# Additions of a two-level Strassen product: bank folding in the first pass, and p7's and the weights' outer sums moved from VectorE to GpSimd

## The chip, the cores and the metric

The kernel runs on one core of a Trainium2 chip. The metric is the device time of one execution in microseconds (us); it is the time of the slowest core, and here there is only one. TensorE multiplies matrices into banks of PSUM, VectorE, ScalarE and GpSimd work on elements, and SyncE issues most of the transfers. GpSimd does not touch PSUM in this kernel: whatever comes from a bank goes through VectorE or ScalarE.

## The reference, cut to what matters

Two layers follow each other over 2048 tokens (8 x 256) of width 512. The first adds to the normalised input a linear attention with 32 heads and a mixture of 16 experts; the second adds a plain attention and a low-rank mixture. The change lies in the first layer's attention, in its projections:

```python
qkv = jax.nn.silu(hidden_states @ qkv_w.T)        # 512 -> 3 * 32 * 128
scores = einsum('bhnd,bhmd->bhnm', cq, ck) * diag_decay
intra = einsum('bhnm,bhmd->bhnd', scores, cv)
xf = xf * rsqrt(mean(xf * xf) + EPS)
gate = jax.nn.sigmoid(hidden_states @ gate_w.T)   # 512 -> 32 * 128
return gate * normed @ out_w.T
```

Everything is in 32-bit floats. The four projections q, k, v and gate are one product of the tokens with a weight matrix of 512 x 16384.

## The kernel before

**Passes, units, halves.** The tokens are taken in two passes (`i` = 0, 1) of 1024 tokens. In each pass there are 8 units (`g`), one for each group of 4 heads, and each unit has two halves (`h`): h = 0 makes q and k, h = 1 makes the gates and v. A half is one large matrix product, tokens by weights.

**Two levels of Strassen.** That product is done by Strassen's scheme in Winograd's form, with seven products in place of eight, on two levels. The outer level has the products p1, p2, p6, p5, p3, p7, p4 (`ORDER`); each is an object `Outer` and is itself made of seven inner products with the same names, done in the order p1, p7, (p3 of the outer product before), p6, p4, p2, p5. So there are 2 x 8 x 2 x 7 = 224 outer products, and each inner one is two matmuls of 128 x 128 x 256 in the code (line 872; the records of the profile show two per matmul). The inner products of one outer product accumulate in three kinds of bank: `ps_a` (two of them), `ps_b` and `ps_e`. p1's sum is copied out of bank a (`c1`) before p6 is accumulated onto it, p6's sum likewise (`c2`) before p5, and p7's sum out of bank e (`c3`) before p4. The copy is `copied` (line 1203), the use of the sums is `result` (line 1212).

**What becomes of a result.** An outer product gives four quarters (`q` = 0 to 3, of 128 x 512). They go into four tiles a, b, c, d: p1 makes a; p2 makes b = a + result; p6 is added to a; p5 makes c = a + result; p3 makes d = c + result; p7 is added both to c and to a; p4 is added to a. When b, d, c and a are whole, `Part.begin` starts what follows for them: the silu (h = 0) or the gate (h = 1) on ScalarE, then scores, the weighing of v, the gating (`gT`, line 1016) and the projection back by `w_out`.

**The third operand.** In three of the four quarters a result is the sum of a bank, a copy of an earlier bank and a tile. In the second pass (`u.i` is 1) the tile is already added when the first bank is copied: VectorE writes bank + tile into `cp` (line 1207, by the helper of line 103), and `result` adds the second bank to it. `folded` (line 1199) says which: p2, p6, p5, p4 with a, p3 with c, but not p4's quarters 0 and 3. In the first pass ScalarE copies the bank (line 1209), VectorE adds the second bank, and GpSimd adds the tile, for p2, p5 and p3 straight onto the new tile (`c<-c`), for p6 and p4 by way of a tile `r` (`c<-c,r`).

**p7.** For each of its quarters a tile r = bank + copy is made; GpSimd adds it to c, and VectorE adds it to a (`add_a`, line 1174). For quarter 1 there is no copy, and r is a copy by ScalarE (line 1235).

**Weights.** In the first pass the sums of the weights that both levels need are made on the way, in the tile `w` of the next outer product, by `weights` (line 824); the result of the inner level is stored, and the second pass loads it. `outer_sum` makes sums over a whole quarter, in two pieces of 128 x 512; p6 has four such additions, p3 and p7 have two each, the others none. `inner_sum` makes four sums of 128 x 256 for each outer product, three on VectorE and the fourth on GpSimd. Each step has the name of an inner product of the current outer product behind which it is issued: the outer sums behind p1 and p7, the inner ones behind p7, p6, p6 and p2.

**What sets the order.** VectorE, ScalarE and GpSimd run in the order in which the program issues (`manual_schedule`). Pieces of other work (scores, projections, experts, table transfers) are put between inner products by `later` and `slot` (lines 877 to 888), and a piece is due a number of slots after the one where it was put. TensorE's order is made by the planner from its own costs. The transfers are issued by SyncE, some by ScalarE, the indirect ones by GpSimd. Tiles come from rings: 5 of `cp`, 4 of `sum` (r), 16 of `S`.

Of the kernel before, what the change touches and what calls it, by code (L numbers as in the profile page):

```python
# [73 lines left out]
def block_kernel(  # L74
# [24 lines left out]
    nc = tc.nc  # L99
    mm = nc.tensor.matmul  # L100

    def tt(o, a, b, op, eng=None):
        (eng or nc.vector).tensor_tensor(o, a, b, op)  # L103
# [298 lines left out]
    def add(o, a, b, eng=None):  # L402
        tt(o, a, b, ALU.add, eng)
# [134 lines left out]
    at = NTT * E  # L538
# [257 lines left out]
    with tc.tile_pool(name="attn", bufs=1) as attn, tc.manual_schedule(engines={mybir.EngineType.Activation, mybir.EngineType.Pool, mybir.EngineType.DVE}):  # L796
# [27 lines left out]
        def weights(i, g, h, p, steps):  # L824

            w = loaded[p].pop(0)
            y = w[:, 0:4]
            v = nc.vector
            pool = nc.gpsimd
            kept = ws[2 * g + h][p]  # L830
            if i == 0:
                latest[p] = y

                def outer_sum(f, o, a, b, n):
                    f(o[:, n : n + 2], a[:, n : n + 2], b[:, n : n + 2], v)

                def inner_sum(f, o, a_, b_):
                    f(w[:, o], w[:, a_], w[:, b_], pool if o == 6 else v)
                    if o == 6:
                        later(6, store)  # L840

                def store():
                    nc.scalar.dma_start(out=kept, in_=w[:, 4 if p in RAW else 1 : 8])

                outer = []
                if p == "p6":
                    w5 = loaded["p5"][0]
                    outer = [(add, w5, w5, w5[:, 4:8]), (sub, y, w5, y)]
                elif p == "p3":
                    outer = [(sub, y, y, latest["p6"])]  # L850
                elif p == "p7":
                    outer = [(sub, y, y, w[:, 4:8])]
                for n, when in ((0, "p1"), (2, "p7")):
                    steps += [(when, partial(outer_sum, *at, n)) for at in outer]
                steps += [
                    (when, partial(inner_sum, *at)) for when, at in (
                        ("p7", (sub, 7, 1, 0)), ("p6", (add, 4, 0, 3)), ("p6", (sub, 5, 4, 1)), ("p2", (sub, 6, 2, 5))
                    )
                ]
            return dict(zip(("p1", "p2", "p4", "p5", "p6", "p3", "p7"), (w[:, n] for n in range(1, 8))))  # L860
# [16 lines left out]
        def later(after, f):  # L877
            pieces.append((now[0] + after, len(pieces), f))
            pieces.sort(key=lambda x: x[:2])
# [292 lines left out]
            places_of.update(a=b, b=d, c=c, d=a)  # L1172

        def add_a(a, r):
            add(a, a, r)

        class Outer:


            def __init__(self, unit, h, p):  # L1180
                self.u, self.h, self.p = unit, h, p
                self.steps, self.added = [], []
                self.following = None
                self.w = weights(unit.i, unit.g, h, p, self.steps)
                self.x = first_x.pop(0) if first_x else tokens(unit.i, p, tc.keep_in_program_order)
# [12 lines left out]

            def folded(self, q):

                return self.u.i and (self.p, q) not in (("p4", 0), ("p4", 3)) and {"p2": "a", "p5": "a", "p6": "a", "p4": "a", "p3": "c"}.get(self.p)

            def copied(self, bank, q):
                c = attn.tile([P, 512], FP, tag="cp", name="cp", bufs=5)
# [7 lines left out]
            def result(self, i, j, bank, c):  # L1212

                u, p, q = self.u, self.p, 2 * i + j
                pool = nc.gpsimd
                a = u.tile(self.h, "a")[:, q]
                made, with_ = dict(
                    p1=("a", None), p2=("b", "a"), p5=("c", "a"), p3=("d", "c")
                ).get(p, (None, None))
                if made:  # L1220
                    o = u.tile(self.h, made)[:, q]
                    if c is None and with_ is None:
                        nc.scalar.copy(o, bank)
                    elif c is None:
                        add(o, bank, u.tile(self.h, with_)[:, q])
                    else:
                        add(o, bank, c)
                        if with_ and not self.folded(q):
                            add(o, o, u.tile(self.h, with_)[:, q], pool)
                elif p != "p7" and (c is None or self.folded(q)):  # L1230
                    add(a, bank, a if c is None else c)
                else:
                    r = attn.tile([P, 512], FP, tag="sum", name="r", bufs=4)
                    if c is None:
                        nc.scalar.copy(r, bank)  # L1235
                    else:
                        add(r, bank, c)
                    if p != "p7":
                        add(a, a, r, pool)
                    else:  # L1240
                        c_ = u.tile(self.h, "c")[:, q]
                        add(c_, c_, r, pool)

                        self.added.append(partial(add_a, a, r))
                        if (i, j) == (1, 1):
                            for n in range(3):
                                later(n, self.added.pop(0)) if n else self.added.pop(0)()
                        elif (i, j) == (0, 1):
                            self.added.pop(0)()
                whole = dict(p2=("b", 0, 0), p3=("d", 0, 1), p7=("c", 1, 1), p4=("a", 1, 0)).get(p)  # L1250
                if whole and (i, j) == (0, 1):
                    Part(u, self.h, whole[1], whole[2], u.tile(self.h, whole[0])).begin()
# [228 lines left out]
        for n, (i, g, h, p) in enumerate(plan):  # L1481
            cur = outers[n]
            u = cur.u
            k = ORDER.index(p)
            at = 2 * (i * NG + g) + h
# [381 lines left out]
```

## Time and profile before

| | |
|---|---|
| three runs | 2711.66, 2715.54 and 2711.70 us, median 2711.7 |
| the profiled execution | 2719.83 us, of which the span is 2718.1 |
| TensorE busy in the span | 2637.7 us (97%) |
| VectorE busy | 1915.6 us (70%) |
| GpSimd busy | 1401.4 us (52%) |
| ScalarE busy | 850.6 us (31%) |
| first pass of the attention | from 131 us to about 1224 us |
| second pass | to about 2380 us |

The profile has one execution. Its groups give, for a line, an engine, an operation and its tiles (out<-in), the number of instructions, their busy time and the mean of one in ns, then the engine's idle time in front of them and what ended it. The table of waits adds up that idle time by who waited and for whom: total in us, times, longest. In the timeline a line has the start and the length in us; equal neighbours are merged (x2). PE is TensorE, PEld its weight loads, DVE VectorE, ACT ScalarE, POOL GpSimd, SP SyncE. Nearly all additions have line 103, a helper, so they are told apart by their tiles and shapes.

### The profile page before, as it was taken

To read this page: it belongs to the slowest core of one execution; us is meant where nothing else is said; L and a number is where in the kernel's file an instruction comes from. 1 tells how busy PE (TensorE), PEld (TensorE's weight loads), DVE (VectorE), ACT (ScalarE), POOL (GpSimd) and SP (SyncE) were. 2 spreads that over 40 slices of the span, in tenths; PEclk is the share of its full clock that TensorE was granted. 3 is DMA by queue.
4 is the path that set the end of the run, shared out by engine and by line. 5 is a ranking of instruction groups with operands and counts; after the bars stand their busy time and mean duration, and the time that the engine had idled before them with its cause. 6 is when DMAs were issued, how large, how long until landed. Compare 5 with 4: busy or idle time off the path is not lost. (4 is left out here: it accounts for less than half of the span.)

```text
span 2718.1 us, 38734 instructions
## 1 busy us (share of the span) xinstructions
PE 2637.7 (97%) x14218; PEld 2296.1 (84%) x14218; DVE 1915.6 (70%) x3193; ACT 850.6 (31%) x1249; POOL 1401.4 (52%) x1294
## 2 busy tenths in 40 slices
PE   8999999999999999999999999999999999989999
PEld 5588888888989898988889888888989888967777
DVE  8697777778787787766556565766666676847663
ACT  4234343434343434332322122222312232321121
POOL 7458686868685857664433334252433443362210
PEclk8999999999999999999999999999999999999999
DMA  6798676767777777776768586867767686533211
GB/s 249 296 382 296 243 284 245 282 244 284 251 276 259 271 274 259 278 281 235 269 228 288 210 296 218 291 236 251 272 228 280 245 302 217 205 118 116 79 48 64
DMA packets 163120, 655.62 MB, mean 241 GB/s; under 512 B 19776, under 2 KB 22336, under 8 KB 160960
## 3 DMA queue, kind: packets, MB, share of 16 engines
q1 hardware_dynamic: 125936, 499.16, 52.1%
q10 hardware_dynamic: 21024, 92.81, 8.4%
q0 software_dynamic: 15968, 61.13, 6.7%
q8 instruction: 115, 1.88, 0.3%
q14 instruction: 77, 0.63, 0.1%
HBM read 512.13 MB, written 143.78 MB: 241 GB/s over the span
## 5 line engine op out<-in xcount | busy, mean ns | idle before, releaser
L872 PE MATMUL ps_a<-xt,w 128*128 128x256 f32 x2688 | 718.5, 382 | 9.9 <-ACT cp L1209 4.0
L872 PEld LDWEIGHTS ps_a<-xt,w 128*128 128x128 f32 x2688 | 470.8, 191 | 67.2 <-issue 10.3
L103 POOL TENSOR_TENSOR c<-c,r 128x512 f32<-128x512 f32 x256 | 352.8, 1393 | 239.9 <-DVE r L103 220.7
L1069 PE MATMUL ps_sc<-wo,gT 128*128 128x256 f32 x1792 | 424.2, 380 | 4.5 <-DVE gT L1016 3.0
L1209 ACT COPY cp<-ps_a 128x512 f32<-128x512 f32 x304 | 177.5, 584 | 676.5 <-PE ps_a L872 582.5
L1069 PEld LDWEIGHTS ps_sc<-wo,gT 128*128 128x128 f32 x1792 | 335.2, 191 | 49.5 <-DVE gT L1016 3.5
L872 PE MATMUL ps_e<-xt,w 128*128 128x256 f32 x1344 | 366.7, 382 | 6.5 <-DVE c L103 6.5
L103 POOL TENSOR_TENSOR sums<-sums,sq 128x256 f32<-128x256 f32 x240 | 195.9, 816 | 327.8 <-ACT sq L1007 318.2
L103 DVE TENSOR_TENSOR w<-w 128x256 f32<-128x256 f32 (+1 forms) x464 | 353.0, 769 | 5.4
L872 PEld LDWEIGHTS ps_a<-w,xt 128*128 128x128 f32 x1792 | 270.5, 191 | 23.0
L872 PE MATMUL ps_a<-w,xt 128*128 128x128 f32 x1792 | 272.2, 274 | 0.0
L103 POOL TENSOR_TENSOR c<-c 128x512 f32<-128x512 f32 x144 | 191.4, 1340 | 146.5 <-DVE c L103 138.2
L872 PEld LDWEIGHTS ps_e<-xt,w 128*128 128x128 f32 x1344 | 232.8, 192 | 32.5 <-DVE c L103 8.0
L103 DVE TENSOR_TENSOR acc<-ps_sc,acc 128x512 f32<-128x512 f32 x196 | 134.7, 688 | 146.5 <-PE ps_sc L1069 145.8
L1016 DVE SCALAR_TENSOR_TENSOR gT<-ps_o,nw,c 128x256 f32<-128x256 f32 x256 | 111.9, 478 | 151.2 <-ACT sq L1007 127.4
L872 PE MATMUL ps_b<-xt,w 128*128 128x256 f32 x672 | 182.6, 380 | 0.0
L103 DVE TENSOR_TENSOR c<-c,r 128x512 f32<-128x512 f32 x128 | 170.9, 1366 | 4.9 <-ACT r L1235 4.9
L103 POOL TENSOR_TENSOR gT<-gT 128x512 f32<-128x512 f32 x128 | 170.3, 1331 | 3.8 <-DVE gT L1016 1.3
L103 DVE TENSOR_TENSOR s<-ps_sc,decay 128x384 f32<-128x384 f32 x256 | 139.9, 552 | 43.0 <-PE ps_sc L984 42.1
L103 DVE TENSOR_TENSOR c<-ps_a,c 128x512 f32<-128x512 f32 x160 | 109.7, 686 | 85.5 <-PE ps_a L872 84.7
L1007 ACT ACTIVATE sq<-ps_o 128x512 f32<-128x512 f32 x128 | 76.6, 599 | 285.3 <-PE ps_o L997 260.7
L996 PE MATMUL ps_o<-s,c 128*128 128x256 f32 x512 | 157.3, 389 | 8.8 <-DVE gT L1016 8.5
(291 smaller groups left out, 4369.5 us busy)
## 6 DMA issues: line engine op xcount, KB each, us to landing
xt<-xc SPq DMA_DIRECT2D x224, 896.0 KB
w<-in_w_att_dram SPq DMA_DIRECT2D x144, 512.0 KB
w<-in_w_att_dram SPq DMA_DIRECT2D x48, 384.0 KB
wo<-in_w_out_dram SPq DMA_DIRECT2D x56, 256.0 KB
decay<-dec SPq DMA_DIRECT2D x32, 384.0 KB
yd<-ye SPq DMA_DIRECT2D x36, 256.0 KB
wos<-wo ACTq DMA_DIRECT2D x32, 256.0 KB
wo<-wos SPq DMA_DIRECT2D x32, 256.0 KB
```

Source lines behind the costliest of these rows:

```text
L103: (eng or nc.vector).tensor_tensor(o, a, b, op)
L872: mm(o, a, b, start=(first and ty == 0), stop=True, skip_group_check=True)
L996: mm(po[:, bass.ts(hh, S)], v[:, 0:P], s[:, 0:S], start=True, stop=False)
L1007: nc.scalar.activation(sq, po, AF.Square)
L1016: nc.vector.scalar_tensor_tensor(gT[:, h, :], po[:, bass.ts(h, S)], nw[:, n : n + 1], self.c[:, 2 * h + t, 0:S], ALU.mult, ALU.mult,)
L1069: mm(py[:, bass.ts(t, S)], self.O[l, p][:, hh, bass.ts(t, P)], self.wo[p][:, hh, :], start=(t == 0 and hh == 0), stop=(hh == 1), skip_grou ...
L1209: nc.scalar.copy(c, bank)
```

## The change

It has four parts. `folded` no longer asks for the second pass, so in the first pass too the third operand is added by VectorE when the first bank is copied. The outer sums of the weights are issued to GpSimd. The additions of p7's results to a are issued to GpSimd, in both passes; and for quarter 1 of p7, where there is no copy, VectorE adds the bank straight to c and then to a, in both passes. For outer products whose weights have outer sums (p6, p3, p7) the inner sums are issued one inner product later: behind p6, p4, p2 and p5.

```diff
-                    f(o[:, n : n + 2], a[:, n : n + 2], b[:, n : n + 2], v)
+                    f(o[:, n : n + 2], a[:, n : n + 2], b[:, n : n + 2], pool)
...
+                whens = ("p6", "p4", "p2", "p5") if outer else ("p7", "p6", "p6", "p2")
                 steps += [
-                    (when, partial(inner_sum, *at)) for when, at in (
-                        ("p7", (sub, 7, 1, 0)), ("p6", (add, 4, 0, 3)), ("p6", (sub, 5, 4, 1)), ("p2", (sub, 6, 2, 5))
+                    (when, partial(inner_sum, *at)) for when, at in zip(
+                        whens, ((sub, 7, 1, 0), (add, 4, 0, 3), (sub, 5, 4, 1), (sub, 6, 2, 5))
                     )
                 ]
...
         def add_a(a, r):
-            add(a, a, r)
+            add(a, a, r, nc.gpsimd)
...
-                return self.u.i and (self.p, q) not in (("p4", 0), ("p4", 3)) and {"p2": "a", "p5": "a", "p6": "a", "p4": "a", "p3": "c"}.get(self.p)
+                return (self.p, q) not in (("p4", 0), ("p4", 3)) and {"p2": "a", "p5": "a", "p6": "a", "p4": "a", "p3": "c"}.get(self.p)
...
                 elif p != "p7" and (c is None or self.folded(q)):
                     add(a, bank, a if c is None else c)
+                elif p == "p7" and c is None:
+                    c_ = u.tile(self.h, "c")[:, q]
+                    add(c_, bank, c_)
+                    add(a, bank, a)
                 else:
```

## Prediction

> **What bounds the kernel now.** I read the stages first: the busy time by stretches, here from 204 us to the end of the first pass at about 1224 us, and the second pass to 2380 us.
>
> ```profile
> core 0: us, PE busy (x) PEld busy (x) DVE busy (x) ACT busy (x) POOL busy (x), PEclk, DMA share, GB/s
> 204.00:1224.00 1020.00, 1002.84 (x5551) 901.58 (x5550) 796.53 (x1216) 394.48 (x573) 729.11 (x659) 1.00 0.75 269
> 1224.00:2380.00 1156.00, 1138.24 (x6516) 1016.90 (x6514) 757.29 (x1159) 315.50 (x436) 455.57 (x430) 1.00 0.71 251
> ```
>
> TensorE is idle 17.2 us of the first pass and 17.8 us of the second. No edit here takes a matmul away, so those gaps are nearly all that can be won. What ends them is in the table of waits of TensorE, first pass and then second:
>
> ```profile
> PE ps_o L996 <- DVE gT L1016: 8.5, 8, 1.4
> PE ps_e L872 <- DVE c L103: 6.5, 8, 1.2
> PE ps_a L872 <- DVE r L103: 1.5, 4, 0.4
> PE ps_sc L983 <- DVE s L103: 6.0, 3, 2.5
> PE ps_sc L1069 <- DVE gT L1016: 3.0, 1, 3.0
> ```
>
> All of these name VectorE, though it is busy only 78% and 66%. So it is late at certain places. The timeline around one gap of each pass shows why. First pass (start, duration, instruction):
>
> ```profile
> 378.03 2.35 DVE L103 TENSOR_TENSOR w<-w 128x256 f32<-128x256 f32 x2
> 378.65 1.45 POOL L103 TENSOR_TENSOR c<-c,r 128x512 f32<-128x512 f32 x1
> 380.13 1.06 ACT L965 ACTIVATE c<-c 128x1024 f32<-128x1024 f32 x1 [4.03 <-POOL c L103]
> 383.69 0.60 ACT L1007 ACTIVATE sq<-ps_o 128x512 f32<-128x512 f32 x1
> 384.32 0.88 DVE L1016 SCALAR_TENSOR_TENSOR gT<-ps_o,nw,c 128x256 f32<-128x256 f32 x2 [1.55 <-ACT sq L1007]
> 385.34 0.73 PE L996 MATMUL ps_o<-s,c 128*128 128x256 f32 x1 [1.37 <-DVE gT L1016]
> ```
>
> Read it upwards: the matmul waits for gT, gT for the square, the square stands behind the gate on ScalarE, and the gate waited 4.03 us for p7's last addition to c on GpSimd. Second pass:
>
> ```profile
> 1413.94 6.78 DVE L103 TENSOR_TENSOR c<-c,r 128x512 f32<-128x512 f32 x2
> 1414.63 4.93 POOL L103 TENSOR_TENSOR c<-c,r 128x512 f32<-128x512 f32 x4
> 1420.64 0.54 DVE L103 TENSOR_TENSOR s<-ps_sc,decay 128x384 f32<-128x384 f32 x1
> 1421.24 0.48 PE L983 MATMUL ps_sc<-c 128*128 128x256 f32 x1 [2.52 <-DVE s L103]
> ```
>
> Two VectorE additions with both operands in SBUF took 6.78 us while GpSimd ran four of its own; alone one takes 0.67 us. The scores stood behind them and a matmul behind those. Additions that read PSUM took 0.68 us beside the same kind of GpSimd work.
>
> **The change part by part.** Groups of the first pass:
>
> ```profile
> L103 DVE TENSOR_TENSOR w<-w 128x512 f32<-128x512 f32 x128 | 124.3, 982 | 1.1
> L103 DVE TENSOR_TENSOR c<-c,r 128x512 f32<-128x512 f32 x64 | 78.0, 1248 | 0.0
> L103 POOL TENSOR_TENSOR c<-c 128x512 f32<-128x512 f32 x144 | 191.4, 1340 | 146.5 <-DVE c L103 138.2 <-issue 8.2
> L1209 ACT COPY cp<-ps_a 128x512 f32<-128x512 f32 x226 | 131.9, 584 | 463.1 <-PE ps_a L872 371.3 <-DMA xr<-x 22.7 <-DVE w L103 22.2
> ```
>
> *Third operand with the first bank (first pass).* Per half 3 copies each in p2, p6, p5, p3 and 1 in p4 become VectorE additions: 13 x 16 = 208, at 0.688 us (the second pass's cp<-ps_a,c) +143 us on VectorE, -122 us on ScalarE (0.585 each). GpSimd loses 144 c<-c (-191 us) and 4 x 16 = 64 additions of r for p6 and p4 (-90 us, 1.40 each); the results that wrote r now write a, at the same price.
>
> *Outer sums to GpSimd.* 128 additions leave VectorE (-124 us) and cost GpSimd 128 x 1.34 = +172 us.
>
> *p7.* 64 additions to a per pass leave VectorE: -78 us and, second pass, 64 x 1.484 = -95 us. Per p7 three go to GpSimd, the fourth quarter is added from its bank twice on VectorE, and one copy of ScalarE and one addition to c go. Per pass: VectorE +32 x 0.688 = +22 us, GpSimd 48 - 16 = 32 more at 1.40, +45 us.
>
> Sums: VectorE -37 us in the first pass and -73 in the second; GpSimd -64 (-191 - 90 + 172 + 45) and +45; ScalarE -131 and -9. Neither engine is the bound by totals, so only lateness counts. SP's order and its DMAs stay; on GpSimd's queue the outer sums now stand among the indirect DMAs of the table (1.02 us each) and wait for weights to land, with c, a and sums behind them. At 131 to 204 us that queue had long gaps.
>
> A rule against the change: the Trainium skill, "GPSIMD Engine Reference", Engine selection, gives elementwise additions to VectorE and calls GpSimd about twice as slow. The trace agrees (1.27 against 0.67 us); by the rule alone the outer sums are a loss of 128 x 0.6 = 77 us, by the stage totals nothing, since GpSimd keeps 29% idle.
>
> What goes on the path:
> - ps_o 8.5 us: c is finished by GpSimd's third addition (374.97 + 1.3 = 376.3) and VectorE's from the bank, so the gate starts some 3 us earlier. 1.37 us of wait is covered twice: -8.5.
> - ps_e 6.5 and ps_a 1.7 (1.5 and a row of 0.2): before 362.96 VectorE had outer sums and others of 3.23 us (357.28); they go: -8.
> - Second pass: additions like 6.78 us above stand before 1421, 1575 and 1730, and one of 5.35 us at 2231 before the wait of 3.0: -9.
> - Slow restart: after 385.34 four matmuls take 1.43 us where 1.03 is usual, and the clock is 0.97 in two stretches of 68 us (about 2 us each): -1.5, between 0 and -4.
>
> What comes:
> - Start: p2's first copy was made by ScalarE at 140.67; VectorE does the routing sums until 144.8, and the product p6 that needs the bank ran about 144: +2, between 0 and +4.
> - Copies behind VectorE's queue: in the bare outer products p6 and p5 of h=1 (ps_b at 472.24, 478.38, 484.30: 6.1 and 5.9 us) VectorE has 7 additions from PSUM at 0.60 us spacing and 3 of weights at 0.43, 5.5 us where it had 3.7. A copy has two products (1.76 us) to be done in and needs about 1. The far end is one blocked addition in SBUF (2.16 us at 349.74, 1.7 over a free one): 16 x 0 to 1.7. I take 0.4, near the second pass, where TensorE barely waits for cp (1.1 us in all): +6.
> - New wait: p4's copy of quarter 2 now needs GpSimd's addition to a. From r at 447.6: three to c, one of weights, one to a = 4 x 1.27 + 0.73 = 5.8, so 453.4; the product that needs the copy starts at 455.61, so 1.5 us are left after the copy's 0.69. Behind the waiting copy stand scores and weights, and p5 on TensorE. At 32 places 0 to 0.7 (one addition blocked 2.16 us ahead of it, less 1.5); I take 0: the 1.5 us that stay are more than the 1.27 of one GpSimd addition.
>
> Sum: -8.5 - 8 - 9 - 1.5 + 2 + 6 = -19. The profiled execution took 2719.8 us (span 2718.1 and 1.7 around it), so 2700.8; the median of the runs is 8.1 lower: **2693 us**.
>
> **Rivals.**
> *Slower: GpSimd's sums block the weights in front of the copies.* In p2, p5 and p3 VectorE's inner sums have both operands in SBUF and now run beside the outer sums that feed them. A blocked one waits for one GpSimd addition, 1.3 us, with a copy behind it; less the slack of about 0.3 that is 1 us of TensorE, at 3 x 16 = 48 places: +48 - 27 (all gains but the start) + 2 = +23: 2735. It decides from 0.5 us at each. For it: w<-w 128x256 at 0.69 on average, not 0.43, and 2.35 for two at 378.03. Against: they start a product later, and of the outer products only two a unit are bare (others take 8 to 16 us).
> The Trainium skill, "SBUF — State Buffer", Who interferes with whom, says that a VectorE instruction with two SBUF inputs and a GpSimd one that reads SBUF exclude each other for a whole instruction. The trace agrees at 1413.94 (6.17 us for the first of two).
> *No gain: the gaps move.* TensorE, no longer held here, comes to weights that have not landed (DMA share 0.75), or the new waits give 20 us back: 2707 to 2717, say 2711. Against: waits for DMA cost it 1.4 us before 204 us and none after in the first pass.
> *It does not do what it says*: the list of instructions shows the 208 and 128 moved; 0.
>
> **Numbers.** Forecast 0.64, no gain 0.13, slower 0.23. A change under 0.2% (5.4 us) can't be told from none here: faster 0.64, same 0.13, slower 0.23. The likeliest case alone spans 2682 (2693 less the 6 and 2 that come and 2.5 more of restart) to 2706; the range goes 4 lower, the spread of the runs shown (2711.66 to 2715.54), to 2678, and up to 2727, most of the way to the slower case, leaving out about 0.1 above and 0.1 below.
>
> **What would show it.** Right: no ps_o<-gT and ps_e<-c waits over 0.5 us from 204 to 1224, no s wait at 1421, ScalarE's L965 not waiting for GpSimd, TensorE idle under 12 us in that pass. Wrong: TensorE waiting for cp in p2, p5, p3, or VectorE's cp for GpSimd's a at p4, over 0.5 us each time; or weights' inner sums over 1 us on average.

## The result, and the profile after

The changed kernel takes 2696.76 us (median of four runs, 2694.35 to 2698.81), the kernel before 2713.19 beside it: a ratio of 0.9938, 95% interval 0.9921 to 0.9956, so 16.4 us faster. Forecast were 2693 us and a range of 2678 to 2727. The profiled execution took 2695.74 us, with a span of 2693.9.

Waits of TensorE in the profile after, the same stretches as before, first the first pass (204 to 1224 us), then the second (total us, times, longest):

```profile
PE ps_e L873 <- DVE c L103: 7.3, 8, 1.1
PE ps_a L873 <- DVE c L103: 1.0, 5, 0.2
```

```profile
PE ps_sc L913 <- DMA xw<-xnd,whose: 8.8, 2, 5.8
PE ps_sc L1070 <- PEq L1324: 1.5, 1, 1.5
PE ps_sc L1070 <- issue: 1.3, 1, 1.3
PE ps_a L873 <- DVE cp L103: 0.4, 1, 0.4
```

The waits for gT and for s are gone. The wait for c in bank e, forecast to go, is there once a unit as before, 7.3 us after 6.5. In these stretches of the first pass TensorE waits for no copy `cp`.

The groups of the first pass that the change touches:

```profile
L103 DVE TENSOR_TENSOR w<-w 128x256 f32<-128x256 f32 x330 | 184.2, 558 | 22.5 <-POOL w L103 17.8 <-DMA ws61p<-w 2.6
L103 DVE TENSOR_TENSOR cp<-ps_a,c 128x512 f32<-128x512 f32 x150 | 103.0, 686 | 37.4 <-PE ps_a L873 31.9 <-POOL w L103 4.7
L103 POOL TENSOR_TENSOR w<-w 128x512 f32<-128x512 f32 x128 | 162.1, 1274 | 16.5 <-DMA w<-in_w_att_dram 13.7
```

The outer sums cost GpSimd 1274 ns each; the inner ones on VectorE are shorter than before (558 after 693 ns), but VectorE now waits for GpSimd in front of some of them: 17.8 us.

For an account by stages I take the starts of TensorE's products into bank b in each profiled execution, which are the same products in every kernel, and subtract those of the profiled execution before:

| | before, us | change after |
|---|---|---|
| first unit of the first pass | 121.0 | +2.5 |
| its units 2 to 8 | 941.4 | -15.6 |
| second pass | 1174.8 | -8.1 |
| all around them | 481.0 | -3.0 |

The last row has none of the changed instructions, and ten of the thirteen changed kernels (this one and those below) are 1.1 to 5.1 us shorter there: the execution of before that was profiled seems to have taken longer in it than usual. So of the 24.2 us between the two spans 21 belong to the change at most. Each stage is from one execution per kernel; differences of a few us in a stage are not shown to be there in the times.

### The profile page after: what moved, and what is told of

The parts are those of the page before. It is cut to its first block, busy times and chain, and to the rows that moved or that the text cites. A ratio compares the mean times of both kernels' runs of the same rounds, so it can differ in the third digit from the quotient of the medians.

```text
span 2693.9 us, 38333 instructions
## 1 busy us (share of the span) xinstructions
PE 2629.2 (98%) x14218; PEld 2295.1 (85%) x14218; DVE 1780.0 (66%) x3209; ACT 713.0 (26%) x1009; POOL 1308.3 (49%) x1278
## 5 line engine op out<-in xcount | busy, mean ns | idle before, releaser
L103 POOL TENSOR_TENSOR c<-c,r 128x512 f32<-128x512 f32 x256 | 322.8, 1284 | 229.0 <-DVE r L103 228.5
L103 POOL TENSOR_TENSOR sums<-sums,sq 128x256 f32<-128x256 f32 x240 | 180.1, 750 | 360.7 <-ACT sq L1008 350.8
L103 POOL TENSOR_TENSOR w<-w 128x512 f32<-128x512 f32 (+1 forms) x240 | 242.3, 1019 | 211.4 <-DVE w L103 178.8
L103 DVE TENSOR_TENSOR cp<-ps_a,c 128x512 f32<-128x512 f32 x288 | 198.1, 688 | 73.3 <-PE ps_a L873 61.6
L1210 ACT COPY cp<-ps_a 128x512 f32<-128x512 f32 x160 | 93.4, 584 | 539.9 <-PE ps_a L873 517.2
L103 DVE TENSOR_TENSOR c<-ps_a,c 128x512 f32<-128x512 f32 x224 | 150.9, 685 | 82.6 <-PE ps_a L873 81.7
L103 DVE TENSOR_TENSOR w<-w 128x256 f32<-128x256 f32 x336 | 186.9, 556 | 22.5 <-POOL w L103 17.8
```

Of the source, the lines that this page charges most:

```text
L1210: nc.scalar.copy(c, bank)
```

## The experiments

Three parts (the fold; p7; the outer sums on GpSimd with their later inner sums) give eight kernels with the two known ones. Each ratio is to runs of the kernel before that were taken beside it, and the last three columns are the differences by stage, as in the table above.

| kernel | ratio (95% interval) | median, us | unit 1 | units 2-8 | second pass |
|---|---|---|---|---|---|
| all (the change) | 0.9938 (0.9921-0.9956) | 2696.8 | +2.5 | -15.6 | -8.1 |
| p7 alone | 0.9884 (0.9868-0.9900) | 2686.3 | -2.9 | -15.2 | -12.3 |
| fold alone | 1.0001 (0.9991-1.0011) | 2715.1 | +0.9 | -1.4 | -1.5 |
| weights alone | 1.0205 (1.0188-1.0222) | 2771.9 | +11.3 | +46.6 | -1.0 |
| without p7 | 1.0011 (1.0000-1.0022) | 2718.7 | +2.9 | -4.3 | -1.1 |
| without the weights | 0.9919 (0.9899-0.9938) | 2692.1 | -0.5 | -13.1 | -14.2 |
| without the fold | 1.0149 (1.0134-1.0164) | 2758.1 | +8.6 | +43.5 | -11.7 |

### p7 alone

```diff
-            add(a, a, r)
+            add(a, a, r, nc.gpsimd)
...
+                elif p == "p7" and c is None:
+                    c_ = u.tile(self.h, "c")[:, q]
+                    add(c_, bank, c_)
+                    add(a, bank, a)
```

> The kernel before with one part alone: p7's additions to a on GpSimd, and quarter 1 of p7 added from its bank to c and to a by VectorE, in both passes. By my theory the second pass loses its waits for s and gT behind VectorE additions with both operands in SBUF (9 us), and the first pass gains a few us at the most where VectorE is relieved of 78 us, since the gate still waits for GpSimd's c: 2713 - 9 - 3 = 2701 us, 2697 to 2707. By the rival that the fold is the gain: 2713 us, and the waits of the second pass only move.

2686.3 us: some 30 us faster than before, faster than the range of 2697 to 2707, and faster than the whole change. The second pass gives 12.3 us where 9 were expected, the first 18 where 3 were. TensorE's waits in its units 2 to 8 (254 to 1224 us) are the wait for bank e and little else:

```profile
PE ps_e L872 <- DVE c L103: 5.3, 7, 1.2
PE ps_a L872 <- DVE c L103: 0.3, 1, 0.3
```

So the wait for gT went with p7's edits, without any fold. The expectation had kept it ("the gate still waits for GpSimd's c"), although the prediction's own step for it rests on quarter 1 being added from its bank, which is part of p7.

### One half of p7, and the other

Quarter 1 direct, with the other additions to a left on VectorE:

```diff
+                elif p == "p7" and c is None:
+                    c_ = u.tile(self.h, "c")[:, q]
+                    add(c_, bank, c_)
+                    add(a, bank, a)
```

> The kernel before with half of the p7 part: quarter 1 of p7 is added from its bank to c and to a by VectorE; p7's other additions to a stay on VectorE. p7's part alone took 29 us. My theory is that its gain in the first pass (18 us) comes from this half: c no longer waits for a copy by ScalarE and an addition by GpSimd, the gate starts earlier, and the wait of TensorE for gT goes with the slow matmuls behind it; its gain in the second pass (12 us) comes from the other half. So about -14 to -18 here: 2699 us, 2695 to 2704. The rival is that the first pass gains by the relief of VectorE from additions in SBUF, most of which stay here: then -5 at the most, 2708 to 2714.

2696.6 us, ratio 0.9929 (0.9915 to 0.9943), within the range expected: these four lines alone give the time of the whole change. By stages: unit 1 -1.9, units 2 to 8 -16.4, second pass -4.1. Its timeline at the place of the gap (start, duration, instruction) shows how the gate is reached:

```profile
375.93 1.28 DVE L103 TENSOR_TENSOR c<-ps_a,c 128x512 f32<-128x512 f32 x2
376.70 1.06 ACT L965 ACTIVATE c<-c 128x1024 f32<-128x1024 f32 x1 [1.56 <-DVE c L103]
```

The gate starts 0.1 us after the first of the two additions from the bank has ended, where before it waited for a copy on ScalarE, a queue on GpSimd and an addition there.

The other half, all four additions to a on GpSimd and quarter 1 as before:

```diff
-            add(a, a, r)
+            add(a, a, r, nc.gpsimd)
```

> The kernel before with the other half of the p7 part: p7's additions to a are GpSimd's, all four quarters, and quarter 1 still goes by way of ScalarE's copy and GpSimd. By my theory the second pass gains its 9 to 12 us (no VectorE addition with both operands in SBUF is left in it to be blocked), and the first pass keeps the wait for gT, perhaps 1 us longer each time, since GpSimd has more to do ahead of c: 2715 - 11 + 4 = 2708 us, 2702 to 2714. By the rival that relief of VectorE is the gain in both passes: 2690 to 2697.

2756.2 us, ratio 1.0147 (1.0130 to 1.0163): some 40 us slower, where 7 less than before was expected. Both theories missed it. Waits of its first pass, units 2 to 8, and the timeline of one:

```profile
PE ps_o L996 <- DVE gT L1016: 23.1, 6, 4.2
PE ps_sc L983 <- ACT c L960: 8.1, 7, 1.3
```

```profile
378.22 5.51 POOL L103 TENSOR_TENSOR c<-c,r 128x512 f32<-128x512 f32 x4
378.37 0.59 ACT L1235 COPY r<-ps_a 128x512 f32<-128x512 f32 x1
383.69 1.53 POOL L103 TENSOR_TENSOR sums<-sums,sq 128x256 f32<-128x256 f32 x2
385.18 4.94 POOL L103 TENSOR_TENSOR c<-c,r 128x512 f32<-128x512 f32 x4
386.48 1.06 ACT L965 ACTIVATE c<-c 128x1024 f32<-128x1024 f32 x1 [6.21 <-POOL c L103]
391.69 0.74 PE L996 MATMUL ps_o<-s,c 128*128 128x256 f32 x1 [4.20 <-DVE gT L1016]
```

The copy of quarter 1 is ready at 378.96, but GpSimd works through four additions and two sums of squares first. The addition that completes c is the first of the four at 385.18, after which the gate starts at 386.48. TensorE waits 4.20 us for gT, until 391.69. The silu of h = 0 waits for GpSimd's c in the same way, and the scores behind it (8.1 us). With quarter 1 direct the gate no longer depends on that queue, and the same move of additions to GpSimd is worth a further 10 us (2686.3 against 2696.6), 8 of them in the second pass: the move pays only behind the other edit.

### The fold alone, the weights alone

```diff
-                return self.u.i and (self.p, q) not in (("p4", 0), ("p4", 3)) and {"p2": "a", "p5": "a", "p6": "a", "p4": "a", "p3": "c"}.get(self.p)
+                return (self.p, q) not in (("p4", 0), ("p4", 3)) and {"p2": "a", "p5": "a", "p6": "a", "p4": "a", "p3": "c"}.get(self.p)
```

> The kernel before with one part alone: the third operand is added by VectorE with the first bank in the first pass too. My theory is that the gain comes from single places, each with its own instruction that is late. By it this part takes away the wait of TensorE for gT (8.5 us), because GpSimd's additions to c go, but the weights' outer sums stay on VectorE, which is then busy 797 + 143 = 940 of 1020 us in the first pass; the wait for c in bank e, 6.5 us now, should grow by about 1 us a unit, and the start costs 3. Sum about +3: 2716 us, between 2700 and 2735, and the second pass unchanged. The rival is that the fold alone is the gain, because it takes 281 us from GpSimd and 122 from ScalarE: then 2697 to 2700 us.

2715.1 us, no difference. TensorE's waits, units 2 to 8:

```profile
PE ps_a L872 <- DVE cp L103: 8.7, 17, 0.7
PE ps_sc L1069 <- POOL gT L103: 7.6, 7, 1.1
PE ps_o L996 <- DVE gT L1016: 0.2, 1, 0.2
```

The wait for gT is gone here too, but gT is no sooner ready. At the place of the gap (this unit begins 1.3 us later than before) the gate still waits 3.27 us for GpSimd's c and starts at 380.74 us, before at 380.13; gT is ready at 386.8, before at 385.2. TensorE comes to it later, at 386.92, having waited elsewhere: 8.7 us for copies and 7.6 us for GpSimd's sums of gT in units 2 to 8. So the wait moved. That in bank e, expected to grow, is gone as well; the total came out near the expected one (2716) with other waits in it.

```diff
-                    f(o[:, n : n + 2], a[:, n : n + 2], b[:, n : n + 2], v)
+                    f(o[:, n : n + 2], a[:, n : n + 2], b[:, n : n + 2], pool)
...
+                whens = ("p6", "p4", "p2", "p5") if outer else ("p7", "p6", "p6", "p2")
```

> The kernel before with one part alone: the weights' outer sums on GpSimd, their inner sums one product later. By my theory GpSimd is then busy 729 + 172 = 901 of 1020 us in the first pass, with the additions to c, a and r behind the outer sums; the gate waits longer for c, and TensorE for gT some 2 us more a unit; the wait for bank e stays, now behind GpSimd. About +15 us: 2728, between 2713 and 2745; second pass unchanged. By the rival that VectorE's total is what counts, relieving it of 124 us gives some 6 us: 2707.

2771.9 us: some 56 us slower, more than the range of 2713 to 2745. Waits of units 2 to 8, TensorE and then VectorE:

```profile
PE ps_a L873 <- DVE c L103: 33.2, 22, 2.8
DVE w L103 <- POOL w L103: 73.3, 30, 5.3
```

The place is another than expected: not the gate behind GpSimd, but VectorE, whose inner sums wait for outer sums in GpSimd's queue, with the emptying of banks behind them.

### The change with one part undone

Without the fold (the line above put back):

> The changed kernel with one part undone: the first pass is not folded (ScalarE copies, GpSimd adds the third operand). By my theory GpSimd is then the late one, at 729 + 172 + 45 = 946 of 1020 us of the first pass: the first pass loses 20 to 40 us against the changed kernel, the second keeps its 9; 2697 + 30 = 2727, between 2713 and 2745. By the rival that the fold only moves work between engines that are not the bound: 2697 to 2701.

2758.1 us, some 60 us above the change: the direction expected, and more than the range. Waits of units 2 to 8:

```profile
PE ps_a L873 <- DVE c L103: 33.4, 22, 2.7
PE ps_e L873 <- DVE c L103: 7.0, 9, 1.1
```

These are the waits of the kernel with the weights' part alone, and VectorE waits 75.8 us for GpSimd's outer sums, where it waits 17.8 in the change. So the fold's worth in the change is that it clears GpSimd's queue for the outer sums: 0 us by itself, some 60 us under them.

Without the weights' part (both edits of `weights` put back):

> The changed kernel with one part undone: the weights' outer sums are VectorE's again and the inner sums stand where they stood. VectorE is then at 797 + 143 - 78 + 22 = 884 of 1020 us in the first pass, GpSimd at 493. By my theory the wait for bank e stays as it is (7.3 us, behind VectorE's own sums in place of GpSimd's), so this part of the change is worth little: 2697 + 3 = 2700 us, 2694 to 2707. By the rival that the relief of VectorE by 124 us matters: 2710 or more.

2692.1 us, below the range of 2694 to 2707. The interval (0.9899 to 0.9938) meets that of the change (0.9921 to 0.9956): the weights' part gives no gain that can be shown, as expected. The reason given was wrong. The wait for bank e did not stay; in units 2 to 8 TensorE has the waits of the fold instead:

```profile
PE ps_sc L1069 <- POOL gT L103: 7.6, 7, 1.1
PE ps_a L872 <- DVE cp L103: 1.9, 4, 0.5
```

Without p7's part (`add_a` on VectorE, quarter 1 by way of r):

> The changed kernel with one part undone: p7's additions to a are VectorE's again, and quarter 1 goes by way of r and GpSimd, in both passes. By my theory the second pass loses its 9 us again (the waits for s and gT come back), and the first pass a few: 2697 + 9 + 3 = 2709 us, 2704 to 2714. By the rival that the second pass's gain was something else in that execution (a transfer): 2697 to 2701.

2718.7 us, some 20 us above the change, where 12 were expected, and above the range of 2704 to 2714: fold and weights together gain nothing. The second pass, -1.1 against -8.1, gives back 7 of the 9 us expected; units 2 to 8 give back 11.3 us, where 3 were expected of the whole first pass. TensorE waits there 5.9 us in 12 places for copies and 1.1 for gT.

### The place of the inner sums

The change with the inner sums where they were, behind p7, p6, p6 and p2:

```diff
-                whens = ("p6", "p4", "p2", "p5") if outer else ("p7", "p6", "p6", "p2")
+                whens = ("p7", "p6", "p6", "p2")
```

> The changed kernel with one part undone: the inner sums of p6, p3 and p7 are issued where they were, behind p7, p6, p6 and p2, with the outer sums still on GpSimd. By my theory the first inner sum then stands on VectorE right behind the issue of the second outer sum, and waits for it (1.27 us and GpSimd's queue) with the copy of quarter 2 and p4's bank behind it: 48 places at 0.5 to 1 us, about +30: 2727 us, between 2715 and 2745. By the rival that only the place in bank e of p7's weights counts, where the wait is there already: 2697 to 2702.

2726.0 us, ratio 1.0039 (1.0024 to 1.0054): the number is as expected, its working is not. It is not 48 places at 0.5 to 1 us. The timeline of one unit:

```profile
367.43 1.27 POOL L103 TENSOR_TENSOR gT<-gT 128x512 f32<-128x512 f32 x1
368.65 2.49 POOL L103 TENSOR_TENSOR w<-w 128x512 f32<-128x512 f32 x2
371.18 0.43 DVE L103 TENSOR_TENSOR w<-w 128x256 f32<-128x256 f32 x1 [3.82 <-POOL w L103]
371.52 0.68 DVE L103 TENSOR_TENSOR c<-ps_a,c 128x512 f32<-128x512 f32 x1
372.30 1.14 PE L872 MATMUL ps_a<-xt,w 128*128 128x256 f32 x3 [2.77 <-issue]
```

One place a unit, p7's weights: VectorE stands 3.82 us for GpSimd's two outer sums, and bank a is emptied behind it. TensorE's matmul follows 0.1 us after that ends; this wait, which the profile gives to "issue", makes 19.4 us in 7 places of units 2 to 8.

The change with p7's inner sums later still:

```diff
-                whens = ("p6", "p4", "p2", "p5") if outer else ("p7", "p6", "p6", "p2")
+                whens = ("p4", "p2", "p2", "p5") if p == "p7" else ("p6", "p4", "p2", "p5") if outer else ("p7", "p6", "p6", "p2")
```

> The changed kernel with p7's inner sums one product later still (behind p4, p2, p2, p5), so that p4's bank e is emptied by VectorE before the sum that waits for GpSimd's outer sums. By my theory the wait of TensorE for c in bank e (7.3 us, 8 times) goes, and the slow matmuls behind it: 2697 - 8 = 2689 us, 2686 to 2693, unless the product p7 of the next outer product then waits for its weights, which I put at 0.3 us each (+2). By the rival that the wait is for the weights themselves and only changes its name: 2697.

2696.6 us, ratio 0.9929 (0.9912 to 0.9947): not to be told from the change, outside the range of 2686 to 2693 and at the rival's number. In the trace the first pass moves in the direction expected: units 2 to 8 are at -19.6, 4 us below the change, and the waits there are

```profile
PE ps_e L873 <- DVE w L103: 1.9, 4, 0.5
PE ps_e L873 <- PE ps_a L873: 1.3, 3, 0.4
PE ps_a L873 <- DVE c L103: 0.8, 4, 0.2
```

So bank e is emptied in time, and 1.9 us of waits for the weights follow. The second pass of that execution, which this edit does not touch, was 7.4 us longer than that of the change. Whether the 4 us are there in the time stays open.

p7 alone, with the inner sums one product later, for p7's weights only and then for all three outer products; the outer sums stay on VectorE:

```diff
+                whens = ("p6", "p4", "p2", "p5") if p == "p7" else ("p7", "p6", "p6", "p2")
```

> The p7 part alone (2686 us), and p7's weights' inner sums one product later, on VectorE as before. In the p7 part alone TensorE waits 0.8 to 1.4 us a unit for VectorE to empty bank e, with two inner sums in front of it on VectorE (0.83 us). By my theory these waits shrink to under 0.3: 2686 - 6 = 2680 us, 2677 to 2684. By the rival that the next wait is for the weights themselves: 2686.

> The p7 part alone (2686 us), and the inner sums of all three outer products with outer sums (p6, p3, p7) one product later, on VectorE as before: the shift as the change makes it, without the move to GpSimd. By my theory it does what the shift of p7's alone does, 2680 us, and some tenths more where other banks wait behind inner sums: 2676 to 2684. By the rival that the later sums of p6, which has four outer sums, come too late for the product that reads them: 2686 to 2694.

2680.6 us, ratio 0.9873 (0.9854 to 0.9891), and 2683.7 us, 0.9886 (0.9871 to 0.9901). Both are faster than the change, and both times lie in the ranges expected. Neither can be told from p7 alone by its interval, but the first pass of the former is 4 us shorter in the trace (units 1 to 8 at -22.0 against -18.2), and the wait for bank e is gone from its units 2 to 8:

```profile
PE ps_sc L1070 <- POOL gT L103: 1.8, 4, 0.5
PE ps_a L873 <- DVE c L103: 1.1, 1, 1.1
```

With all three later the first pass is at -18.9. The wait for bank e is gone there too, but 6.3 us of waits for bank a have come in 6 places. At one of them, 306.0 us, bank a is emptied behind an inner sum that took 2.37 us (from 302.89) beside GpSimd's additions.

## Why the prediction was right or wrong

The time was 4 us off and the sign right, but several steps were wrong, and they cancelled: 8 us forecast for banks e and a did not come, and neither did 6 us of cost for the copies, while the restart gave 6 us more than forecast. That the number came so near is luck in part. Of the signs named beforehand, the waits for gT and s are gone, the gate waits no longer for GpSimd, and TensorE is idle 8.3 us between 204 and 1224 us; but the waits for c in bank e, which were to stay under 0.5 us, go up to 1.1. (For the 2706 at the top of the likeliest case the prediction shows no working.)

**ps_o, -8.5: right.** The wait is gone, and by the step named: c's quarter 1 no longer waits for GpSimd. Four lines do that alone. The prediction did not say that this step belongs to the p7 part and needs nothing of the fold and the weights, and so did not see that the rest was not needed.

**ps_e and ps_a, -8.2: failed for the most part.** "They go": the sums did leave VectorE, the wait stayed. The timeline after, once a unit:

```profile
361.07 1.27 POOL L103 TENSOR_TENSOR gT<-gT 128x512 f32<-128x512 f32 x1
361.25 0.60 PE L873 MATMUL ps_e<-xt,w 128*128 128x256 f32 x2
362.30 2.50 POOL L103 TENSOR_TENSOR w<-w 128x512 f32<-128x512 f32 x2
364.82 0.42 DVE L103 TENSOR_TENSOR w<-w 128x256 f32<-128x256 f32 x1 [2.63 <-POOL w L103]
365.17 0.68 DVE L103 TENSOR_TENSOR c<-ps_e,cp 128x512 f32<-128x512 f32 x1
365.90 0.70 PE L873 MATMUL ps_e<-xt,w 128*128 128x256 f32 x2 [0.97 <-DVE c L103]
```

Bank e is full at about 362.3. VectorE, next in its order, has the inner sum of p7's weights, which waits for both outer sums: the second reads w[6:8], and the inner sum writes w[7]. GpSimd gets to them only after sums of squares and gT. So VectorE idles 2.63 us, the addition that empties bank e runs behind it, and TensorE waits 0.97. The cost was shifted from VectorE's time to its waiting, in front of the same instruction. The prediction gave the inner sums a product's delay and asked only what a blocked one costs, not when GpSimd would have finished what they read.

**Second pass, -9: right** in its waits (9.0 us of s and gT are gone) and near in its length (-8.1; -12.3 in p7 alone). Of the change, 3.5 us went to a longer wait for the experts' gather, 8.8 after 5.3 us; it is 3.8 to 8.8 us in the profiles of all these kernels. The two halves of p7 do it only together: -4.1 and +4.7 alone.

**Slow restart, -1.5 (0 to -4): too small.** In units 2 to 8 the intervals between matmul starts are, summed over what exceeds the usual, some 30 us before and 15 after. Of the difference of 15.6, 8.2 are waits of over 0.35 us; 4.1 are intervals 0.15 to 0.35 too long, and they go entirely; 3.3 are smaller ones, whose cause is open. So -7.4 stands where -1.5 was put, of which the slow matmuls are 4.1. The row that the prediction read, a clock of 0.97 over two stretches of 68 us, gives 2 us for each, 4 in all; that far end is what came, and for taking 1.5 it gave only four matmuls behind one gap. After the gap at 385.34, in two stretches of before (busy times by engine, then the granted clock):

```profile
core 0: us, PE busy (x) PEld busy (x) DVE busy (x) ACT busy (x) POOL busy (x), PEclk, DMA share, GB/s
384.00:386.00 2.00, 0.66 (x2) 0.60 (x3) 1.68 (x4) 0.76 (x2) 2.00 (x3) 0.85 0.95 315
386.00:388.00 2.00, 2.00 (x9) 1.72 (x7) 0.37 (x1) 0.00 (x0) 1.92 (x3) 0.50 1.03 419
```

**Start, +2 (0 to +4): right in size, half in its cause.** The first unit is 2.5 longer. It is 2.9 shorter with p7 alone, 0.5 shorter with the fold added (so the fold costs some 2.5), and 2.5 longer with the weights added (3.0 more). The latter was not foreseen. From the timeline after, VectorE and GpSimd:

```profile
140.51 2.67 POOL L103 TENSOR_TENSOR w<-w 128x512 f32<-128x512 f32 x2 [13.69 <-DMA w<-in_w_att_dram]
140.86 2.60 DVE L103 TENSOR_TENSOR disp<-disp 128x256 f32<-128x256 f32 x2
143.98 3.67 DVE L103 TENSOR_TENSOR disp<-disp 128x64 f32<-128x64 f32 x4
144.81 2.62 POOL L103 TENSOR_TENSOR w<-w 128x512 f32<-128x512 f32 x2
148.31 2.07 PE L873 MATMUL ps_b<-xt,w 128*128 128x256 f32 x4 [3.06 <-DVE c L103]
```

Before, the same routing sums took 0.89 and 0.62 us with no outer sum on GpSimd beside them. They have both operands in SBUF, bank b is emptied behind them, and TensorE waits 3.06 us. The Trainium skill, "SBUF — State Buffer", Who interferes with whom, says that such a VectorE instruction and a GpSimd one that reads SBUF exclude each other; the trace agrees, with 2.60 and 3.67 us. The prediction had weighed this for the weights' own sums and not for the routing's.

**Copies behind VectorE's queue, +6 (0 to 27): did not come.** No wait of TensorE for a copy by VectorE is in the first pass after. What keeps it out is p7's part in the main. With the fold but without p7's part the wait is there in units 2 to 8, at 8.7 us in 17 places with the outer sums on VectorE and 5.9 in 12 with them on GpSimd; with p7's part it is 1.9 in 4 places, and 0. In 13 of the 17 and in all of the 12 one of p7's additions to a, of 0.68 or 1.75 us, stands on VectorE shortly before the copy. The prediction looked at the additions from PSUM and the weights in front of the copies, and not at these, which its own change takes away. The other 4 places go with the outer sums.

**New wait at p4, 0: right**; no wait of TensorE follows from it.

**Engine totals.** Over the first pass (from 131 us, 5747 matmuls in each) VectorE fell by 74 us, GpSimd by 118 and ScalarE by 128; forecast were 37, 64 and 131. Counts and prices held; in addition the two-operand sums became shorter, the inner sums alone by 44 us. None of this is the gain: the fold alone takes GpSimd from 686 to 441 us between 254 and 1224 us and moves the time by nothing.

**Rivals.** The slower one's mechanism exists, at one place a unit and not at three a half: with the inner sums not shifted the kernel is slower than before (2726.0 us). The shift is what kept it out, by some 28 us. Transfers did not become the limit of the first pass: no wait of TensorE for a DMA is in it.

## What to carry to other kernels

Find the instruction that a gap waits for and take it off the queue it stands in; here four lines for one quarter gave what the whole rebalancing gave, and moving p7's additions to a to GpSimd was worth -10 or +40 us according to whether those lines were there. When work is moved to another engine, ask when that engine will reach it and who stands behind the consumer: an in-order engine that waits for a result blocks everything behind it as surely as if it had done the work itself. Parts that were changed together can be worth nothing or harm alone: the outer sums on GpSimd cost some 56 us without the fold, the fold moved nothing without them, and both together gained nothing over neither; put on top of p7's part they cost some 10 us (2696.8 against 2686.3).

## What the runs showed of the hardware

The clock after a gap was not a matter of its length alone. Before, the matmul that ends the gap was 1.53 us late at 385, 521 and 792 us, and 1.54 at 658; behind the first two the next matmuls started 0.43 us apart in place of 0.22 (granted clock 0.50 from 386 to 388), behind the other two at their usual pace. Gaps of 1.14 us in the profile after had no slow matmul behind them. The Trainium skill, "TensorE: Matmul & The Clock Gate", Part 1: The HAM clock gate (the "warmup" mystery), has the clock fall to half after at least one idle window of about 3.4 us, and lets the windows run freely. That 1.37 us of idle time sufficed does not fit an idle window, and here the measurement decides. That equal gaps fared differently does fit windows that run freely. The granted clock, as the trace records it, begins to be low at 385.38 and 521.92 us and is full again from 388.80 and 525.33; in every trace here its changes lie on one grid of 3.41 us. Four steps of this grid, in the columns shown above:

```profile
381.97:385.38 3.41, 1.66 (x10) 1.04 (x8) 1.86 (x5) 2.76 (x5) 3.41 (x4) 1.00 0.94 323
385.38:388.80 3.42, 3.42 (x10) 2.92 (x11) 0.99 (x2) 0.56 (x1) 2.92 (x4) 0.50 1.03 418
655.03:658.44 3.41, 1.94 (x11) 1.68 (x12) 1.86 (x5) 2.03 (x4) 3.41 (x4) 1.00 0.87 273
658.44:661.86 3.42, 3.42 (x19) 3.03 (x19) 2.13 (x5) 2.37 (x4) 3.26 (x5) 1.00 0.90 333
```

In the first of them TensorE is idle 1.75 us, the gap and a smaller one before it, and half clock follows; before 521.92 it is 1.74. In the step that holds the gap at 658 it is 1.47 us, and the gap at 792 is cut in two by an edge of the grid (1.18 and 0.58): no half clock follows. Over the fourteen profiles, from 150 to 2380 us, half clock followed every step of full clock with more than 2 us idle and none with less than 1.7; in between it sometimes did. So what counted here was about half a step of idle time, added up within the step.
